# A two-layer graph attention kernel: the first layer's step with row-tiled turns and 64x64 columns

## The chip, the cores and the metric

The kernel runs on one core of a Trainium2 chip. A core has a matrix engine (TensorE, PE in the profile; its weight loads are PEld), VectorE (DVE), ScalarE (ACT), GpSimd (POOL) and SyncE (SP), which work side by side and wait for each other by semaphores. Matrix products land in PSUM, eight banks of 512 float32 columns on 128 partitions; everything else lives in SBUF or in the chip's memory, reached by DMA. The metric is the device time of one execution in microseconds.

## The reference

Eight graphs share one 2048 x 2048 adjacency matrix; every node has 64 features. Two attention layers follow one another, and a node attends only to its neighbours and itself. Then come two normalisations.

```python
def _gat_layer(h, mask, b):
    scores = jnp.einsum('...nd,...md->...nm', h, h)
    scores = jnp.where(mask, scores, NEG)
    attn = jax.nn.softmax(scores, axis=-1)
    return jnp.einsum('...nm,...md->...nd', attn, h) + b

mask = graph + jnp.eye(N) > 0
h = jnp.einsum('bnc,hdc->bhnd', x, Wh)               # 4 heads of 64
out_h = _gat_layer(h, mask, bh)                      # first layer
z = leaky_relu(concat of heads, 0.2)
h2 = jnp.einsum('bnk,dk->bnd', z, Wo)
out2 = _gat_layer(h2, mask, bo)                      # second layer
z2 = leaky_relu(out2, 0.2)
out = layernorm(z2) * gamma + beta
return layernorm(x + out)
```

The adjacency is sparse away from the first nodes: node i is linked to node j with a probability that falls with both numbers.

## The kernel before, in words

**Sets.** The first 56 nodes, the hubs, are dense and are handled against all nodes in an opening stage (0 to about 150 us). The other 1992 nodes are cut into 166 sets of 12. For each set the kernel finds at most 128 nodes that are neighbours of any of the 12 (the list of the set), and then works densely on 128 x 12 with a mask. Lists are found in three rounds of 60, 60 and 46 sets: `make_keys` turns adjacency bits into numbers, `pick` (L727) selects the 128 largest by VectorE instructions MAX8 and MATCH_REPLACE8 (`top`, L735), eight at a time, and `members` builds the masks. `pick` returns a list of jobs; `some(n)` runs the next n of them.

**The first layer's step.** 83 pairs of sets, g = 0 to 82. The loop at L1017 runs over i and each pass emits the work of several pairs at different depths of the pipeline; this order in the code is the order on each engine, since the schedule is written by hand. In pass i before the change:

- scores of pair i+1 (L814, L821): 32 products of 64x64 by 48 columns, each two passes of TensorE (a float32 product is always two, a turn one); then the mask is subtracted on VectorE (`weigh`, L826);
- the projection of pair i-1 by head (L531, 16 passes), and its bias on ScalarE (`leaky`, L518);
- ScalarE copies the turned rows of pair i+2 out of PSUM (L1030), then takes the exponential of pair i+1 (`lift`, L833);
- values of pair i (L846, 32 passes, 128 rows by 64 columns), then on VectorE the reciprocals of the sums and their product with the values (`invert`, L853 and L854);
- POOL issues two gathers (L792), one for each list, of 128 rows from a table in memory for pair i+5, and every second pass copies own features of the sets to come (`own_rows`, L800);
- the leaky part of pair i-1 on VectorE (`leak`, L523); the second layer's features of pair i-2 (`second_maps`, L880) and their copy (`keep_own`, L885); the turn of pair i-3's features into rows (`second_rows`, L890), their bias (`keep_rows`, L894) and the write to the second layer's table (L897);
- columns (L806): own features of pair i+4 multiplied by each head's Gram matrix; two products of the full 128x128 array with 192 columns, in which the Gram matrix stands twice on the diagonal; ScalarE keeps them (L812);
- the turns (L512, L863): the gathered rows of pair i+3, two times four turns of 128x128, and between the two the turn of pair i's values, four of 112x128, copied by ScalarE in two instructions (L870).

PSUM holds four tiles of two banks, one of each kind: S (scores), C (`cat`: projection, columns, second maps, second rows), O (values and their turn) and T (turned rows). A tile is taken again only when its readers have finished, and where two engines read one bank, they do so in turn.

**Selection.** Rounds two and three of `pick` run beside the first layer's step, one or two jobs a pass; a job is a MAX8 and its MATCH_REPLACE8 together. Passes below zero run none. Three more hub jobs for each of two halves (`hub_later`, L622) and the key making of round three also lie in the first passes.

**The second layer** works in 42 groups of four sets on the table that the first layer wrote: gather of 128 rows for each set (L792), the same turn (L512 from `turn2`, L1314), a copy (L1320), scores (L1133), exponential (L1136), a turn of scores (L1144), mask (L1152), values (L1165) and the normalisations on VectorE and ScalarE. The hub stage turns x with the same function (`turn_x`, L580).

## Time and profile before

| what | us |
|---|---|
| median of 14 runs | 1043.41 (1039.75 to 1050.45) |
| the profiled execution | 1040.47 |
| its span | 1038.5 |
| hub stage (to the first step's products) | 0 to about 150 |
| first layer: first scores to last scores, 83 of them | 156.4 to 612.7 |
| second layer, from the last write of rows | 629 to 1038.5 |

The busy line of the page gives each engine's busy time, its share of the span and its instructions. A line of the chain of work that ended last has the start, the length and the engine, tile and line of a piece; "issue" is time in which nothing visible was waited for, and "remote" in a timeline is a releaser that the profile couldn't name. A timeline line has start, length, engine, line, operation, output and inputs, shapes, count, and in brackets the idle time ahead of it with what ended it. PE busy counts overlapping products once.

### The profile page before, as it was taken

What the parts mean: (1) busy time and instruction counts of PE and PEld (TensorE: products, weight loads), DVE (VectorE), ACT (ScalarE), POOL (GpSimd) and SP (SyncE); (2) the same over time, 40 slices, a digit from 0 to 9 for tenths busy, and PEclk for the clock granted to TensorE, in tenths of its full rate; (3) what the DMA queues carried; (4) which work ended last, traced back from release to release, by engine and by line L of the source; (5) the groups of instructions that cost most, each with busy time, mean ns of one, the idle gap of its engine ahead of it and who ended that gap; (6) DMA issues with size and microseconds to landing.
All of it is one profiled execution on the core that took longest, in us unless ns stands there. A gap on an engine that the chain in (4) does not pass through costs nothing.

```text
span 1038.5 us, 42066 instructions
## 1 busy us (share of the span) xinstructions
PE 828.6 (80%) x18437; PEld 697.1 (67%) x18437; DVE 612.7 (59%) x1369; ACT 518.6 (50%) x961; POOL 462.9 (45%) x612
## 2 busy tenths in 40 slices
PE   3976779899999999999999983577787787777740
PEld 2654457778899888888888973366576665655540
DVE  3449735688777777555555553024454555557695
ACT  2322235555666666666666651245444544545541
POOL 6542224563444556555555515444444343545400
PEclk9999889999999999999999996799989899999985
DMA  8885513553444555555555415455555555555521
GB/s 190 230 216 153 149 26 101 151 135 95 107 115 115 144 156 150 155 144 158 149 148 153 131 33 162 141 158 151 157 158 164 150 161 151 164 159 159 164 60 32
DMA packets 81794, 145.22 MB, mean 140 GB/s; under 512 B 30146, under 2 KB 46466, under 8 KB 81602
## 3 DMA queue, kind: packets, MB, share of 16 engines
q0 software_dynamic: 26720, 88.55, 31.5%
q1 hardware_dynamic: 37842, 49.65, 16.4%
q10 hardware_dynamic: 17040, 4.25, 2.3%
q8 instruction: 147, 2.41, 1.0%
q14 instruction: 45, 0.37, 0.1%
HBM read 123.91 MB, written 18.48 MB: 137 GB/s over the span
## 4 chain that ended last, share of the span: by engine, by line
PE 65%; DVE 10%; issue 8%; ACT 7%; DMA 3%; another core or an unknown queue 3%; POOL 2%; SPq 0%; DVEq 0%; POOLq 0%; ACTq 0%
PE t L512 15%; PE s L821 10%; PE o L846 8%; PE cat L806 5%; PE s L1133 4%; PE cat L531 3%; PE o L863 3%; ACT xTg L1320 3%; PE o L1165 3%; PE cat L880 3%; PE sh L1277 2%; PE e L1144 2%; PE cat L890 2%; DMA x<-in_x_dram 1%
## 5 line engine op out<-in xcount | busy, mean ns | idle before, releaser
L792 POOL DMA_INDIRECT g<-table,index x332 | 330.1, 994 | 404.6 <-PE o L846 171.9
L512 PE MATMUL t<-ident,g 128*128 128x128 f32 x1328 | 200.6, 281 | 25.2 <-DMA gh<-table 10.8
L512 PEld LDWEIGHTS t<-ident,g 128*128 128x128 f32 x1328 | 158.8, 145 | 44.4 <-issue 36.7
L1320 ACT COPY xTg<-t 128x1024 f32<-128x1024 f32 x83 | 80.6, 1016 | 129.5 <-PE t L512 81.4
L826 DVE TENSOR_TENSOR e<-s,mask 128x768 f32<-128x768 f32 x83 | 79.4, 957 | 105.3 <-PE s L821 104.7
L821 PE MATMUL s<-y,xTg 64*64 64x48 f32 x5312 | 114.6, 222 | 4.9 <-issue 3.8
L821 PEld LDWEIGHTS s<-y,xTg 64*64 64x64 f32 x5312 | 98.6, 134 | 24.5 <-issue 16.2
L1152 DVE TENSOR_TENSOR es<-e,linked 128x384 f32<-128x384 f32 (+1 forms) x42 | 23.1, 550 | 137.3 <-PE t L512 84.8
L518 ACT ACTIVATE z<-cat,bhp 128x192 f32<-128x192 f32 x166 | 60.7, 417 | 86.0 <-PE cat L531 86.0
L846 PE MATMUL o<-g,e 128*64 128x65 f32 x2656 | 97.4, 227 | 0.0
L846 PEld LDWEIGHTS o<-g,e 128*64 128x64 f32 x2656 | 85.8, 140 | 10.0 <-issue 0.4
L1133 PE MATMUL s<-xTg,bd 128*32 128x128 f32 x1328 | 62.8, 303 | 33.0 <-issue 20.6
L1030 ACT COPY xTg<-t 128x1024 f32<-128x1024 f32 x83 | 84.0, 1012 | 1.9 <-PE t L512 1.9
L833 ACT ACTIVATE e<-e,shifts 128x768 f32<-128x768 f32 x83 | 79.2, 954 | 2.0 <-DVE e L826 2.0
L1133 PEld LDWEIGHTS s<-xTg,bd 128*32 128x32 f32 x1328 | 41.5, 120 | 49.7 <-issue 39.7
L597 ACT ACTIVATE e<-e,shifts 128x896 f32<-128x896 f32 x32 | 33.4, 1042 | 80.5 <-DVE e L594 69.2
L812 ACT COPY y<-cat 128x384 f32<-128x384 f32 (+1 forms) x80 | 40.7, 509 | 64.2 <-DVE rowt L894 42.3
L806 PE MATMUL cat<-xo,gram 128*128 128x192 f32 (+1 forms) x320 | 65.0, 326 | 0.0
L680 POOL TENSOR_SCALAR a<-raw 120x1024 bf16<-120x1024 int32 (+1 forms) x34 | 38.1, 1123 | 59.0 <-DMA raw<-in_adj_dram 31.2
L853 DVE RECIPROCAL rall<-o 64x8 f32<-64x8 f32 x166 | 34.1, 205 | 45.4 <-PE o L846 43.9
L1165 PE MATMUL o<-g,es 128*32 128x65 f32 x2656 | 54.3, 234 | 7.8 <-DVE y_s L1188 5.1
L854 DVE TENSOR_TENSOR osb<-o,rall 128x512 f32<-128x512 f32 x83 | 57.3, 691 | 2.9
(177 smaller groups left out, 1440.3 us busy)
## 6 DMA issues: line engine op xcount, KB each, us to landing
raw<-in_adj_dram SPq DMA_DIRECT2D x32, 480.0 KB
table<-xb SPq DMA_DIRECT2D x22, 256.0 KB
xr_s<-table SPq DMA_DIRECT2D x21, 256.0 KB
g<-table,index POOLq DMA_INDIRECT x332
table<-x SPq DMA_DIRECT2D x16, 260.0 KB
x<-in_x_dram ACTq DMA_DIRECT2D x32, 128.0 KB
table<-rowt SPq DMA_DIRECT2D x166, 24.4 KB
xb<-in_x_dram SPq DMA_DIRECT2D x164, 24.0 KB
```

Of the source, the lines that this page charges most:

```text
L512: nc.tensor.transpose(tp[:, q * P:(q + 1) * P], rows[:, q, 1:1 + P], ident)
L518: nc.scalar.activation(z[:, hp], cat[:, :, hp * n:(hp + 1) * n], AF.Identity, bias=bhp[:, hp:hp + 1], scale=1.0)
L792: nc.gpsimd.indirect_dma_start(out=t.rearrange("n q c -> n (q c)"), out_offset=None, in_=table, in_offset=bass.IndirectOffsetOnAxis(ap=ind ...
L806: nc.tensor.matmul(cat[:, k, 2 * GM:2 * GM + n], gram[:, g % 2 * 2 + k, :], held["x", g // 2][:, :n], start=True, stop=True)
L821: nc.tensor.matmul(sp[half(r), p, (q * 2 + j) * M:(q * 2 + j + 1) * M], xt[half(p), j, q, half(r)], y[half(p), (j * Q + q) * M:(j * Q + q ...
L826: nc.vector.tensor_tensor(e[:, :16 * M].rearrange("p (a q n) -> p a q n", a=2, q=Q), sp[:, :, :8 * M].rearrange("p a (q n) -> p a q n", q= ...
L833: nc.scalar.activation(e[:, :16 * M], e[:, :16 * M], AF.Exp, bias=shifts[:, 0:1], scale=1.0)
L846: nc.tensor.matmul(op[half(p), j, o0:o0 + K1], e[:, c0:c0 + 64], rw[j][:, q, sums(p)], start=True, stop=True)
L1030: nc.scalar.copy(t, held.pop(("tp", i + 2)))
L1133: nc.tensor.matmul(sp[q * 32:(q + 1) * 32, k, :], bd[u % 3][:, k, q, :], xt[:, s % 2, q, :], start=True, stop=True, tile_position=(0, q * 32))
L1165: nc.tensor.matmul(op[t * 32:(t + 1) * 32, f, k * W2 + p:k * W2 + p + K1], e[:, 2 * q + p, k, :], rw[:, q, sums(p)], start=(a == 0 and k = ...
L1320: nc.scalar.copy(t, tp)
```

## The change

- `turn` is row-tiled: each turn of 128 rows becomes two of 64 rows, one in each half of the array's rows, which write 64 columns each to the two banks of the tile. It is used by the first layer's step, by the hub stage and by the second layer; their readers are adapted.
- Columns are computed in 64x64 tiles without the doubled Gram matrix, 8 products of 96 columns (16 passes) instead of 2 of 192 (4 passes). They move to the O tile, just ahead of the values; `own_rows` lays own features out in two halves with partitions exchanged, by three copies instead of one.
- The turn of values moves from its own pass to the next one, to the C tile behind the projection, in 8 turns of 48 rows instead of 4 of 112; ScalarE copies it in one instruction. What follows (projection, leak, second maps, second rows) moves one pass later too, and the loop has one pass more.
- Second maps go to the S tile, behind the subtraction of the mask. The row turn becomes two turns of 64 rows.
- A selection job is split in two, MAX8 and MATCH_REPLACE8. The hub stage runs six instead of three at a time. In the step: six a pass below pass 0, three a pass up to pass 15 and two from then on, one of them between the subtraction and the leak, the others at the end of the pass behind `keep_rows`.
- Loads of own rows and their beta start at pass 10, in every third pass, instead of at pass 30 in every second.
- Order of a pass now: scores; copy of turned rows; projection; mask, exponential; columns; values; gathers; own rows; one job; second maps; leak; keep own; keep columns; invert; turn of values; second rows; keep values; keep rows; jobs; turns of gathered rows.

```diff
-    def turn(tp, rows):
+    def turn(tp, rows, j=0):
         for q in range(Q):
-            nc.tensor.transpose(tp[:, q * P:(q + 1) * P], rows[:, q, 1:1 + P], ident)
+            c0 = (j * Q + q) * 64
+            for r in range(2):
+                nc.tensor.transpose(tp[:, r, c0:c0 + 64], rows[half(r), q, 1:1 + P], ident[half(r), half(r)])
...
         def top(src, dst, last):
-            def job():
-                nc.vector.max(out=dst, in_=src)
-                if not last:
-                    nc.vector.match_replace(out=src, in_to_replace=dst, in_values=src, imm_value=-1.0)
-            return job
+            todo.append(lambda: nc.vector.max(out=dst, in_=src))
+            if not last:
+                todo.append(lambda: nc.vector.match_replace(out=src, in_to_replace=dst, in_values=src, imm_value=-1.0))
...
     def own_rows(m):
-        w = min(4, NS - 4 * m)
         t = held["x", m] = work.tile([P, 2 * GM], F32, tag="xo", name=f"xo{m}", bufs=2)
-        src = xT[:, :, HUB:].rearrange("c q (k s) -> c s q k", s=NS)[:, 4 * m:4 * m + w]
-        nc.gpsimd.tensor_copy(t[:, :w * 48].rearrange("c (s q k) -> c s q k", s=w, q=Q), src)
+        v = t.rearrange("c (b s q k) -> c b s q k", b=2, s=2, q=Q)
+        src = xT[:, :, HUB:].rearrange("c q (k s) -> c s q k", s=NS)
+        nc.gpsimd.tensor_copy(v[:, 0], src[:, 4 * m:4 * m + 2])
+        b0 = min(4 * m + 2, NS - 2)
+        for r in range(2):
+            nc.gpsimd.tensor_copy(v[half(r), 1], src[half(1 - r), b0:b0 + 2])
-    def columns(g, cat):
-        n = min(4, NS - 4 * (g // 2)) * 48
+    def columns(g, op):
+        t = held["x", g // 2]
         for k in range(2):
-            nc.tensor.matmul(cat[:, k, 2 * GM:2 * GM + n], gram[:, g % 2 * 2 + k, :], held["x", g // 2][:, :n], start=True, stop=True)
+            for r in range(2):
+                for p in range(2):
+                    nc.tensor.matmul(op[half(p), r, Q * OW + k * GM:Q * OW + (k + 1) * GM], gram[half(r), g % 2 * 2 + k, half(r)],
+                                     t[half(r), (p ^ r) * GM:((p ^ r) + 1) * GM], start=True, stop=True)
...
-    def turn_values(g, op):
-        osb = held.pop(("o", g))
+    def turn_values(g, pt):
+        osb = held.pop(("o", g)).rearrange("a j q c -> a (j q c)")
         for w in range(4):
-            nc.tensor.transpose(turned(op)[:, w, :], osb[:112, w].rearrange("a s c -> a (s c)"), ident[:112, :112])
-    def keep_values(g, op):
+            for p in range(2):
+                mine = slice(p * 64, p * 64 + M)
+                nc.tensor.transpose(pt[:, p, w * M:(w + 1) * M], osb[mine, w * P:(w + 1) * P], ident[mine, mine])
+    def keep_values(g, pt):
         ot = held["ot", g] = work.tile([P, H, GM], F32, tag="ot", name=f"otb{g}")
-        v = turned(op)
-        for p in range(2):
-            nc.scalar.copy(ot.rearrange("c h (p w n) -> c p h w n", p=2, w=4)[:, p],
-                           v[:, :, p * 64:p * 64 + M].rearrange("c w (n h) -> c h w n", h=H))
+        nc.scalar.copy(ot.rearrange("c h (p m) -> c p m h", p=2), pt.rearrange("c p (m h) -> c p m h", h=H))
...
     def second_rows(g, pr):
-        nc.tensor.transpose(pr, held.pop(("own", g)), ident)
+        t = held.pop(("own", g))
+        for r in range(2):
+            nc.tensor.transpose(pr[:, r, :], t[half(r)], ident[half(r), half(r)])
...
-    for i in range(-4, NG + 3):
+    for i in range(-4, NG + 4):
...
         cat = one(f"cat{i}", "C")
+        if 0 <= i - 2 < NG:
+            project(held.pop(("ot", i - 2)), cat, GM)
+            held["z", i - 2] = leaky(cat, GM, f"z{i - 2}")
         if 0 <= i + 1 < NG:
+            weigh(i + 1, sp)
             lift(i + 1)
+        op = one(f"o{i}", "O")
+        if 0 <= i + 4 < NG + NG % 2:
+            columns(i + 4, op)
         if 0 <= i < NG:
             values(i, op)
...
+        quota = 6 if i < 0 else 3 if i < 16 else 2
+        if not turns():
+            some(1)
+            quota -= 1
+        if 0 <= i - 3 < NG:
+            second_maps(i - 3, sp[:, 0, 384:384 + GM])
+        if 0 <= i - 2 < NG:
+            leak(held["z", i - 2])
+        if 0 <= i - 3 < NG:
+            keep_own(i - 3, sp[:, 0, 384:384 + GM])
+        if 0 <= i + 4 < NG + NG % 2:
+            keep_columns(i + 4, op)
+        if 0 <= i < NG:
+            invert(i, op)
+        if 0 <= i - 1 < NG:
+            turn_values(i - 1, cat[:, :, 2 * GM:4 * GM])
+        if 0 <= i - 4 < NG:
+            second_rows(i - 4, cat[:GM, :, 384:448])
+        if 0 <= i - 1 < NG:
+            keep_values(i - 1, cat[:, :, 2 * GM:4 * GM])
+        if 0 <= i - 4 < NG:
+            keep_rows(i - 4, cat[:GM, :, 384:448])
+        for _ in range(quota):
+            if not turns():
+                some(1)
...
+            for j in range(2):
+                turn(tp, rows[1, 2 * (i + 3) + j], j)
```

## The prediction

> **What bounds the kernel now.** I read the busy line of the page first, then busy time by stage, then the chain that ended last inside one step of the first layer, then the weight loads by shape, and last one stretch of the second layer.
>
> ```profile
> PE 828.6 (80%) x18437; PEld 697.1 (67%) x18437; DVE 612.7 (59%) x1369; ACT 518.6 (50%) x961; POOL 462.9 (45%) x612
> ...
> 262.00:600.00 338.00, 331.84 (x8581) 298.97 (x8579) 217.02 (x557) 216.24 (x437) 184.16 (x241) 1.00 0.52 141
> 629.00:1038.50 409.50, 271.37 (x5248) 220.12 (x5248) 215.91 (x393) 181.42 (x321) 163.21 (x166) 0.87 0.52 145
> ```
>
> The second and third lines are stretches of the span: PE, PEld, DVE, ACT, POOL busy, then clock, DMA share, GB/s. The 80% is a mean of two regimes. In the first layer's steps (262 to 600 us) TensorE is busy 98% at full clock; VectorE and ScalarE 64%, DMA 52%. In the second layer (from 629) TensorE is at 66%.
>
> One step of the first layer, along the chain that ended last (start, us, what):
>
> ```profile
> 310.59 1.27 PE s L821 x60
> 311.85 0.39 PE cat L531 x16
> 312.24 1.08 PE o L846 x32
> 313.32 0.33 PE cat L880 x8
> 313.65 0.24 PE cat L890
> 313.90 0.65 PE cat L806 x4
> 314.55 0.44 PE t L512 x4
> 314.99 0.39 PE o L863 x4
> 315.37 0.44 PE t L512 x4
> ```
>
> Nothing but TensorE: scores, projection, values, second maps, row turn, columns, and the turns of gathered rows around the turn of values. They add to 5.23 us, and the next scores start 5.22 us later. So here a TensorE microsecond saved is worth one, until another loop is longer.
>
> **The change, part by part.** *Price of a row-tiled turn.* A 128-column turn (L512) takes 0.44/4 = 0.109 us and one of 112 columns (L863) 0.39/4 = 0.097: 0.85 ns a moving column. A matmul is two passes: L806's 0.65/4 = 0.163 us for 192 columns is the same rate. A half turn streams 64 columns, 0.055 us, but still loads 128 stationary columns. The weight loads (min/median/max ns):
>
> ```profile
> L512 PEld LDWEIGHTS t<-ident,g x1328: 137/141/243, 152.2 to 992.3; 128*128 128x128 f32 x190
> ...
> L890 PEld LDWEIGHTS cat<-ident,own x83: 122/124/157, 185.9 to 626.7; 128*96 128x96 f32 x83
> ...
> L846 PEld LDWEIGHTS o<-g,e x2656: 132/138/231, 160.3 to 619.2; 128*64 128x64 f32 x190
> ...
> L806 PEld LDWEIGHTS cat<-xo,gram x320: 186/190/312, 161.8 to 606.8; 128*128 128x128 f32 x160
> ...
> 602.35 0.44 PE t L512 x4
> ...
> 606.73 0.42 PE cat L806 x4
> ```
>
> For turns the load grows from 122 to 137 ns between 96 and 128 columns, about 0.45 ns a column: 128 cost some 0.06 us. For matmuls it grows from 132 to 186 between 64 and 128, 0.84 ns a column; there it can bind: four passes of only 96 columns (the last line) still took 0.42 us. So a half turn costs about 0.058 us, stream and load alike. The two halves lie in different rows of the array and write different banks. That such pairs overlap is shown by the scores: 64 passes of 64x64 in 1.08 us in the step at 603.65, 0.017 each, impossible one after the other with 48 columns at 0.85 ns (0.041). No 64x128 pair is in the trace. Ends: 0.058 a pair (full overlap) and 0.116 (none). I take 0.058, the scores being the nearest row.
>
> [...]
>
> *TensorE's step anew.* Scores 1.28, projection 0.38, values 1.08 and maps 0.33 stay. Columns become 16 passes of 64x64 by 96, the form of the projection: 0.36 (was 0.65). Turn of values: 8 half turns, 4 pairs, 0.23, plus the change of array form that now falls before them (L890, one pass, took 0.24 against 0.11 streamed: 0.13): 0.36 (was 0.39). Row turn: one pair, 0.06 (was 0.24). Gathered rows: 8 pairs, 0.47 (was 0.88). Sum 4.32 us; 0.91 less.
>
> *What is late next: a loop through VectorE.* The O tile is now written by columns and values, read by ScalarE (columns kept) and then VectorE (inversion); readers of one bank go in turn, as L812 waits for L894 today. So each step has: subtraction of the mask 0.96 (L826), exponential 0.95 (L833, next in ScalarE's order), columns kept 0.51 (L812), inversion 0.42 + 0.69 (L853, L854), rows kept 0.28 (L894), the selection jobs at the step's end, and the next subtraction behind them on VectorE. With hand-overs of 0.05 (values end 313.32, L853 starts 313.37) that is 4.0 us, plus 0.49 for each trailing half job (a MAX8 and its replacement start 0.97 apart from the next pair): 4.0, 4.5 or 5.0 with none, one or two. The job between subtraction and leak is beside the exponential.
>
> Jobs: round two of the selection has 66 half jobs, round three 65. 24 go in the four steps before step 0, 48 in steps 0 to 15 (three each), the other 59 at two a step, to about step 45. So: 15 intervals at 5.0, 30 at 4.5, 37 at 4.32 (TensorE) = 370 us; 82 at 5.23 are 429. **-59 us.** What stands above 5.23 now (82 intervals between first and last scores, 156.4 to 612.7, are 456 us, 27 more: hub jobs, key making, short gaps inside the scores) I leave standing; all of it going would be -27, twice it +27.
>
> *Queues.* ScalarE: 1.01 + 0.73 + 0.95 + 0.51 + 0.51 (one copy of values' turn for two) = 3.7 us, under the step. POOL: two gathers 2.0 and their 0.3 gaps, own rows 0.28, column rows three copies every second step (0.53 becomes some 0.9), beta 1.28 in every third step instead of every second from step 10: 3.5 at most. SP issues what it did, own rows' loads 20 steps earlier. Gathers: both issued after the values, needed two steps later at the turns; 10 us of cover become 7. The two of 313.5 and 314.8 had their packets done by 318.1, 3.3 us after the second. If that cover went, each microsecond late would be a microsecond a step.
>
> *Small parts.* The turn of values moves a step later: one step more at the end, a drain of 2 to 4 us by the last intervals (4.4 to 5.0) less what overlaps: **+2.5**. Turning x in the hub stage: 16 x 0.2 off TensorE, busy 69% there: 0 to -3, **-1**. Signals from TensorE that come late (below): 0 to 0.5 us a step; I take 0.05: **+4**.
>
> *Second layer.* It uses the same turn: 83 x 0.41 = 34 us less TensorE work. Is it on the path?
>
> ```profile
> 830.18 2.47 PE L512 MATMUL t<-ident,g 128*128 128x128 f32 x16
> ...
> 832.95 0.94 POOL L792 DMA_INDIRECT g<-table,index  x1 [0.30 <-issue]
> ...
> 833.87 1.93 ACT L1320 COPY xTg<-t 128x1024 f32<-128x1024 f32 x2 [3.17 <-PE t L512]
> ...
> 837.32 2.32 PE L512 MATMUL t<-ident,g 128*128 128x128 f32 x16
> ...
> 839.62 0.94 POOL L792 DMA_INDIRECT g<-table,index  x1 [0.30 <-issue]
> ...
> 841.53 1.93 ACT L1320 COPY xTg<-t 128x1024 f32<-128x1024 f32 x2 [3.67 <-remote]
> ```
>
> The turns end at 832.65 and 839.64, yet the copy behind them starts 1.2 and 1.9 us later, each time when the fourth gather has been issued (833.89, 840.56). The gathers' series, which waits for the values, covers the turns. Ends 0 and -34; I take **-3**.
>
> **Sum.** -59 + 2.5 - 1 + 4 - 3 = -56.5. The profiled execution took 1040.47 us (span 1038.5), so 984; the median, 1043.41, stands 2.9 above it: **987 us**.
>
> **The rivals.** *Row tiles take turns.* Thirteen pairs a step at 0.116 instead of 0.058 are 1.51 us, with the 3.43 that stays or is columns and the 0.13 for the change of form 5.07: 82 x 0.16 = -13, with drain, signals and no gain elsewhere 1034 against the execution, 1037 against the median. For: no 64x128 pair in the trace. Against: the scores.
>
> *A longer loop.* If TensorE's signals come 0.5 us late at each step, subtraction and inversion shift and every interval is near 5.0: 82 x 0.23 = -19, about 1023. For: the second layer's late copies, when gathers are issued. Against: in the first layer at 313.32 the signal took 0.05.
>
> *The second layer gains too.* Were its turns on the path, -31 more: 956. For: the chain names L512 there. Against: the four lines above.
>
> *Slower.* A half turn pays a matmul's load, 0.84 ns x 128 = 0.107 us, and the halves do not overlap: 26 half turns a step are 2.78 us instead of 0.75, the step 6.34: 82 x 1.11 = +91 in the first layer, up to 83 x 0.83 = +69 in the second, so 1134 to 1203 by the median. It decides from the price where the first layer's step passes 5.2: 3.43 + 0.13 + 26 x price, so from 0.063 us for each half turn (half a pair, 0.029, is the forecast). For: L806's loads. Against: L512's.
>
> **How the numbers follow.** Forecast 0.69, its own range 965 to 1005 (the 27 us of excess by half either way, some second layer); second layer too 0.08; row tiles in turn 0.08; longer loop 0.06; slower 0.07; 0.02 is left for no change. 950 to 1030 takes in the first, second and fourth of these, some 0.8, and leaves out the slower case and the row tiles in turn. About 0.3% is what a measurement of this kernel can tell from no change. Row tiles in turn is on the edge of that bound, so a little of it counts as same. Faster 0.90, same 0.03, slower 0.07.
>
> **What would show it.** Right: first-layer scores every 4.3 to 5.0 us, shorter after step 45; eight turn passes in pairs, 16 in about 0.47; L806's successor near 0.36; VectorE as releaser of project (its cat tile) in the first 45 steps; second-layer stretch within 10 us of 409. Wrong: 16 half turns in 0.9 or more; steps above 5.0; TensorE waiting on gathers.

## The result, and the profile after

The changed kernel took 1148.99 us (median of 10 runs, 1144.59 to 1158.74), the kernel before 1043.7 (47 runs): a ratio of 1.101, 95% interval 1.098 to 1.104. It is 10% slower where 5% faster was forecast.

The first lines are the page's busy line and the first line of its chain; then the answer by stretches (span, then PE, PEld, DVE, ACT, POOL busy with instructions, clock, DMA share, GB/s), all of the changed kernel:

```profile
PE 841.4 (73%) x21252; PEld 697.4 (61%) x21252; DVE 617.3 (54%) x1369; ACT 568.6 (49%) x878; POOL 486.5 (42%) x696
...
PE 53%; issue 13%; DVE 11%; ACT 9%; another core or an unknown queue 7%; DMA 4%; POOL 1%; SPq 1%; ACTq 0%; DVEq 0%; POOLq 0%
```

```profile
262.00:600.00 338.00, 280.59 (x8513) 245.07 (x8513) 190.95 (x478) 215.62 (x315) 169.11 (x253) 0.92 0.43 118
750.80:1107.80 357.00, 265.77 (x5652) 215.27 (x5651) 179.83 (x322) 166.81 (x297) 137.98 (x142) 0.83 0.52 141
```

From 262 to 600 us TensorE was busy 331.8 us before; now it is 280.6, though only 52 steps begin in this stretch instead of 63. The step got longer, and every engine is now idle more than before. The granted clock in this stretch fell too, from 1.00 to 0.92. "issue", time in which the engine waited for nothing that the profile shows, went from 8% of the chain to 13%.

By stage (starts of the scores in the two profiled executions): the stretch from first to last scores grew from 456.3 to 531.7 us (median step 5.34 to 5.89), its start moved from 156.4 to 160.8, the passage from the last scores of the first layer to the first of the second grew from 37.4 to 58.3, the second layer's own stretch from 347.3 to 357.0, the tail from 41.1 to 43.1. That is +75, +4, +21, +10 and +2: the 112 us of the two spans.

One step in the chain that ended last (start, us, what):

```profile
405.56 0.33 PE s L888 x8
405.89 0.38 PE cat L874 x8
406.27 0.06 PE cat L900 x2
406.33 0.49 PE t L514 x16
406.82 0.61 PE s L834 x14
407.44 0.41 issue
407.85 0.35 PE s L834 x4
408.20 0.42 issue
408.62 0.88 PE s L834 x42
```

The prices are those forecast: 16 half turns 0.49 (forecast 0.47), turn of values 0.38 (0.36), row turn 0.06; the columns, 16 passes, took 0.33 a few steps later (0.36). But the scores are torn: after 14 passes TensorE stands for 0.41 us, does four passes, stands again. It waits for no semaphore there. In 262 to 600 us the records of the weight loads show 134 such gaps of over 0.15 us, 69.5 us together, 120 of them beginning within 1.3 us of the issue of a gather, moments that make up 40% of the time. Before the change there were 27, 8.1 us together, 2 of them behind a gather. The clock goes with it: it was granted at 0.50 in spells of 3.4 us or more, and the 14 steps of this stretch that such a spell touched took 8.1 us in the mean, the 38 others 5.8. Whether the clock fell because TensorE stood was not tested.

Two more lines of interest, from the page's groups and then POOL's timeline (in brackets the idle time ahead, and what ended it):

```profile
L879 ACT COPY otb<-cat 128x384 f32<-128x384 f32 x83 | 69.6, 839 | 31.3 <-PE t L514 25.2
L808 POOL COPY xo<-xT 64x96 f32<-64x96 f32 x84 | 35.9, 427 | 107.8 <-DMA g<-table,index 102.7
...
L823 ACT COPY y<-o 128x384 f32<-128x384 f32 x80 | 68.6, 857 | 19.8 <-PE o L858 18.0
```

```profile
442.30 1.15 POOL L797 DMA_INDIRECT g<-table,index  x1 [1.75 <-PE o L858]
443.76 0.95 POOL L797 DMA_INDIRECT g<-table,index  x1 [0.30 <-issue]
444.71 0.36 POOL L805 COPY xo<-xT 128x96 f32<-128x96 f32 x1
447.70 0.84 POOL L808 COPY xo<-xT 64x96 f32<-64x96 f32 x2 [2.64 <-DMA g<-table,index]
448.60 0.26 POOL L894 COPY own<-own 128x96 f32<-128x96 f32 x1
```

The exchanged copies of own rows (L808) wait until the gathers issued just ahead have landed: 2.6 us in the mean every second step, in which POOL does nothing. The straight copy L805 just ahead of them does not wait for the gathers. The two ScalarE copies take 0.86 and 0.84 us, where 0.51 was forecast for each.

At the passage to the second layer, from the timeline:

```profile
734.44 1.12 PE L514 MATMUL t<-ident,g 64*128 64x64 f32 x16 [4.17 <-issue]
...
742.96 0.94 POOL L797 DMA_INDIRECT g<-table,index  x1 [0.30 <-issue]
...
747.87 1.93 ACT L1334 COPY xTg<-t 128x1024 f32<-128x1024 f32 x2 [12.78 <-remote]
```

24 gathers follow one another there, the last issued by 743.9. TensorE's turns end at about 735.5, and the copy that needs them starts only at 747.87; ahead of these turns TensorE itself stood 4.2 us for "issue".

### The profile page after: what moved, and what is told of

The parts are those of the page before. It is cut to its first block, busy times and chain, and to the rows that moved or that the text cites. A ratio compares the mean times of both kernels' runs of the same rounds, so it can differ in the third digit from the quotient of the medians.

```text
span 1150.9 us, 47469 instructions
## 1 busy us (share of the span) xinstructions
PE 841.4 (73%) x21252; PEld 697.4 (61%) x21252; DVE 617.3 (54%) x1369; ACT 568.6 (49%) x878; POOL 486.5 (42%) x696
## 4 chain that ended last, share of the span: by engine, by line
PE 53%; issue 13%; DVE 11%; ACT 9%; another core or an unknown queue 7%; DMA 4%; POOL 1%; SPq 1%; ACTq 0%; DVEq 0%; POOLq 0%
PE s L834 11%; PE o L858 8%; PE t L514 7%; PE s L1147 4%; PE cat L537 3%; PE o L816 3%; ACT xTg L1334 3%; PE cat L874 2%; PE sh L1291 2%; DMA raw<-in_adj_dram 2%; PE o L1179 2%; PE s L888 2%; PE e L1158 2%; PE oh L615 1%
## 5 line engine op out<-in xcount | busy, mean ns | idle before, releaser
L797 POOL DMA_INDIRECT g<-table,index x332 | 322.9, 973 | 376.8 <-PE o L1179 155.4
L834 PE MATMUL s<-y,xTg 64*64 64x48 f32 x5312 | 147.2, 231 | 56.6 <-issue 55.4
L514 PE MATMUL t<-ident,g 64*128 64x64 f32 x2656 | 137.6, 239 | 59.7 <-issue 43.6
L834 PEld LDWEIGHTS s<-y,xTg 64*64 64x64 f32 x5312 | 120.5, 142 | 78.7 <-issue 71.0
L514 PEld LDWEIGHTS t<-ident,g 64*128 64x128 f32 x2656 | 111.5, 149 | 81.6 <-issue 72.5
L858 PE MATMUL o<-g,e 128*64 128x65 f32 x2656 | 113.2, 244 | 6.0 <-issue 5.9
L858 PEld LDWEIGHTS o<-g,e 128*64 128x64 f32 x2656 | 99.5, 156 | 19.3 <-issue 11.5
L879 ACT COPY otb<-cat 128x384 f32<-128x384 f32 x83 | 69.6, 839 | 31.3 <-PE t L514 25.2
L808 POOL COPY xo<-xT 64x96 f32<-64x96 f32 x84 | 35.9, 427 | 107.8 <-DMA g<-table,index 102.7
L823 ACT COPY y<-o 128x384 f32<-128x384 f32 x80 | 68.6, 857 | 19.8 <-PE o L858 18.0
L1179 PEld LDWEIGHTS o<-g,es 128*32 128x32 f32 x2656 | 61.3, 138 | 8.3 <-issue 5.5
```

The source lines that it names most:

```text
L514: nc.tensor.transpose(tp[:, r, c0:c0 + 64], rows[half(r), q, 1:1 + P], ident[half(r), half(r)])
L797: nc.gpsimd.indirect_dma_start(out=t.rearrange("n q c -> n (q c)"), out_offset=None, in_=table, in_offset=bass.IndirectOffsetOnAxis(ap=ind ...
L823: nc.scalar.copy(held["y", g // 2].rearrange("p (b n) h -> p b h n", b=2)[:, :, h0:h0 + 2, :], op[:, :, Q * OW:Q * OW + 2 * GM].rearrange( ...
L834: nc.tensor.matmul(sp[half(r), p, (q * 2 + j) * M:(q * 2 + j + 1) * M], xt[half(p), r, j, q, :], y[half(p), c0:c0 + M], start=True, stop=True)
L858: nc.tensor.matmul(op[half(p), j, o0:o0 + K1], e[:, c0:c0 + 64], rw[j][:, q, sums(p)], start=True, stop=True)
L879: nc.scalar.copy(ot.rearrange("c h (p m) -> c p m h", p=2), pt.rearrange("c p (m h) -> c p m h", h=H))
```

## The experiments

They ran on five other chips, on which the kernel before takes 878 to 880 us, not 1043. Each ratio is therefore to the kernel before on the same chip. On these chips the second layer's stretch is 215 us instead of 347, and the first layer's step of the kernel before is a flat 5.00. So they tell what the change does there; what the first result adds is taken up at the end of this section.

### First question: is it the gathers, and what of them?

Three kernels with 156 of the first layer's 166 gathers changed; all three also put a constant in place of the exponentials' argument and never set the final flag, so that only their times are to be read. In the first the gathers are left out:

```diff
+        if layer == 1 and s >= 10:
+            t = rows[layer, s] = fixed[s % 10]
+            return
```

> The changed kernel, in which the first layer gathers only its first 10 lists and reads those ten tiles again and again; the exponential there is taken of a constant so that sums stay finite, and the fallback flag is never set. Left out: 156 of 166 gathers of the first layer. Theory S (starved by gathers): TensorE's issue gaps of 0.4 us inside the scores come while a gather is generated or lands; without gathers they vanish and the step falls from 6.5 us (531.7 us from first to last scores) to 4.3 to 5.0: 360 to 410 us from first to last scores. Theory R (mean rate): TensorE gets some 50 instructions a microsecond whatever else runs (50.8 before, 50.4 after, from 262 to 600 us); then the step stays near 6.4 and the stretch near 525.

In the second SyncE moves as many bytes in a plain transfer, in the third POOL makes the same gather of 64 bytes a row:

```diff
+            nc.sync.dma_start(out=t.rearrange("n q c -> n (q c)"), in_=table[s * 11:s * 11 + P, :])
...
+            nc.gpsimd.indirect_dma_start(out=t.rearrange("n q c -> n (q c)")[:, :16], out_offset=None, in_=tiny,
+                                         in_offset=bass.IndirectOffsetOnAxis(ap=index[:, s:s + 1], axis=0))
```

> As a_gather_none, but in place of each gather left out SyncE issues one plain DMA of the same 128 rows' size (266 KB, consecutive rows of the table) into the same tile. Left out: the choice of rows. If the gather hurts TensorE by the descriptors that POOL generates, the gaps are gone as without gathers: first to last scores 360 to 410 us. If it hurts by its traffic, the gaps stay: above 470 us. Theory R: near 525.

> As a_gather_none, but each gather left out is replaced by an indirect DMA of the same 128 indices that brings 64 bytes a row in place of 2080 (from a small table written in the hub stage). [...] If POOL's descriptors starve TensorE, the stretch from first to last scores stays above 470 us; if the traffic does, it falls to 360 to 410 us. Theory R: near 525.

Measured, one execution each: 884.5, 922.3 and 882.5 us beside 880.3 for the kernel before; stretch of the scores 420, 455 and 426, so neither theory's figures came true. A plain transfer of the same bytes costs some 30 to 35 us of the stretch, and the gathers on POOL with 64 bytes a row next to nothing (6 us of the stretch, none of the time). That POOL makes descriptors, as two expectations have it, is shown by no run; the traces show its gather instruction, 0.97 us each in the changed kernel (L797). But without gathers the step is still 4.87 in the median, not 4.32. Its chain:

```profile
443.95 0.64 PE o L864 x22
444.59 0.16 PE s L894 x3
444.75 0.48 issue
445.23 0.41 PE s L894 x5
445.64 0.38 PE cat L880 x8
446.01 0.06 PE cat L906 x2
446.08 0.49 PE t L514 x16
446.57 1.08 PE s L840 x64
447.64 0.35 PE cat L537 x16
447.99 0.33 PE o L822 x16
448.32 0.20 PE o L864
448.52 0.73 issue
```

The first stop is behind the third pass of the maps, the next behind the first pass of the values, so between them lie 5 + 8 + 2 + 16 + 64 + 16 + 16 + 1 = 128 passes. A pass is two instructions, a weight load and a product (21,252 of each on the changed kernel's page). Counted over 300 to 600 us, 43 of the 44 gaps of over 0.15 us without a wait stand at the same place of a count by 256 instructions. The page's table of DMA queues (packets, MB, share) gives the other half; first the kernel before, then the changed one, both as first measured:

```profile
q8 instruction: 147, 2.41, 1.0%
```

```profile
q8 instruction: 168, 2.75, 1.0%
```

A packet has 16,384 bytes in the records. The 36,874 and 42,504 instructions of TensorE's passes, taken 256 at a time, are 144 and 166, within three of the 147 and 168 packets. From these counts and the place of the gaps I infer that TensorE's program is fetched 256 instructions at a time, a packet each, and that here it runs out. From one such packet, a fetch, to the next it takes at the least 3.2 to 3.5 us in every kernel's first layer (300 to 600 us: 3.74 in the median without gathers, 4.07 with them in the changed kernel on another chip). I call this theory F. A step of the changed kernel has 324 instructions (274 before): 324/256 x 3.74 = 4.73 us, and beside gathers 5.15.

The kernel before on these chips has no such gap at this place from 262 to 560 us; the changed one stops there at 30 of some 69 fetches, 0.17 to 1.95 us each.

### Undoing the row-tiled turns, alone and in the kernel before

All turns of rows whole again, the rest of the change kept:

```diff
-            for r in range(2):
-                nc.tensor.transpose(tp[:, r, c0:c0 + 64], rows[half(r), q, 1:1 + P], ident[half(r), half(r)])
+            nc.tensor.transpose(tp[:, j, q * P:(q + 1) * P], rows[:, q, 1:1 + P], ident)
```

> The changed kernel with the turns of 128 rows undone in all three stages (128x128 again), all else as changed. By its busy time TensorE's step is 4.32 + 0.41 = 4.73 us. Theory S: eight passes of 0.11 us each cover a gap in the supply as sixteen of 0.03 do not; the step falls from 6.5 to 5.0 to 5.6 and the second layer goes back to within 10 us of before: 1010 to 1070 us in all. Theory R: 308 instructions a step instead of 324 at 50 a microsecond, 6.1 us: the first layer gives back 25 us and the second 30: 1090 to 1100.

924.9 us, ratio 1.048 (1.044 to 1.052), the second layer 217.7. Both theories had been given in times of the first result, so the total decides between neither. The median step of 5.25 is no better than the 5.28 of the changed kernel below, though a step has 16 instructions fewer: the turns stream longer again (1.02 us a step where they took 0.49), and TensorE also waits for POOL's exchanged copies of own rows (13.5 us from 262 to 560). On another chip the changed kernel itself, the kernel before, and the kernel before with only the row-tiled turn:

> The changed kernel itself, on the chip of this call, where the kernel before took 880 us in the call before this one instead of 1043. If TensorE's supply is what slows the change (theory S), a chip on which the second layer's steps are faster with the same code should show fewer issue gaps and a ratio nearer to 1: 0.95 to 1.06. If the change is slower for a reason inside the step that has nothing to do with the chip's state (a longer loop through ScalarE and VectorE), the ratio stays at 1.10.

> The kernel before itself, for its profile on the same chip as the others of this call. Both theories: first-layer steps of 5.2 us where TensorE binds.

> The kernel before with one part of the change: row-tiled turns of 128 rows in all three stages, all else as before. TensorE's step is 0.41 us shorter by busy time. Theory S: the queue's stock of long passes shrinks from 12 turns of 0.11 us to 16 half turns of 0.03, so issue gaps show in the scores and the step gets no shorter than 5.2 or longer; without supply trouble on this chip it is 4.9 and the first layer gains up to 30 us. A loop elsewhere: no gain and no gaps.

The changed kernel took 930.3, ratio 1.056 (1.049 to 1.064), with irregular steps (median 5.28, mean 5.73) and the second layer at 225.0 against 215.4. The kernel before repeated itself: 880.1, steps of 5.00. With the row-tiled turn alone it took 896.9, ratio 1.017 (1.009 to 1.024): the step became 5.05. Eight half turns took 0.39 us where four whole ones took 0.44, twice a step, but the turn of values between them, its own form unchanged, went from 0.39 to 0.53; I put that down to the other form of the turns around it, which was not tested by itself. The second layer lost 10 us. The change, then, is slower by 5 to 6% there too, and row-tiled turns are a loss to the second layer.

Where TensorE stands in the changed kernel on this chip can be read from its weight loads. From 262 to 560 us there are 30 stops without a wait at one place of the 256 instructions, 19.5 us, and waits for the exchanged copies of own rows, from the answer on waits (sum, times, longest in us):

```profile
PEld o L816 <- POOL xo L808: 17.8, 26, 2.8
```

The kernel before has neither. That is 0.36 and 0.33 us a step, in steps whose mean grew from 5.05 to 5.46: the shorter streaming makes up for a part only. In the second layer there are 13 stops at that place, 11.2 us, and with the row-tiled turn alone 15, 14.6 us, where the kernel before has one of 0.7: of the size of the 10 us lost.

### Supply measured by itself

Two series of 1536 products of 64x64 by 8 columns behind all work of the kernel before:

```diff
+        for k in range(n):
+            r, p = k % 2, k // 2 % 2
+            nc.tensor.matmul(ps[half(p), r, 0:8], ident[half(r), half(p)], ident[half(r), 0:8], start=True, stop=True)
```

> The kernel before, with two series of 1536 matmuls of 64x64 by 8 columns behind all its work, which change nothing of the output; 24 gathers of 128 rows are issued beside the second series. 3072 instructions a series are 12 fetches of 16 KB in the records of the instruction queue. Theory F (TensorE's instructions come 256 at a time, one fetch after the other, and the shortest distance seen between two fetches is 3.3 us): the first series takes 12 x 3.4 to 3.8 = 41 to 46 us, the second 12 x 4.0 to 4.4 = 48 to 53 us or more. Without such a limit: at most 1536 x 0.017 (the scores' pass, which has more columns) = 26 us, both series alike. Theory S (TensorE starves while gathers land): first series 26 us, second 50 or more.

The expectation had forgotten that each of these products is two passes (768 products were 1,534 in the records of the second kernel's first series, below): each series is 24 fetches, not 12. In the records of weight loads TensorE stood at a multiple of 128 passes again and again, 0.24 to 0.52 us each time before the gathers and up to 1.06 beside them; 20 lots of 256 instructions took 74.9 us, 3.75 each, before the gathers, and 8 lots took 32.7, 4.09 each, beside them. A second kernel measured four series, small products alone and beside 24 gathers, then 400 whole turns alone and beside 24 gathers.

> The kernel before with four series behind all its work, which change nothing of the output: 768 matmuls of 64x64 by 8 columns (1536 passes, 3072 instructions, 12 fetches) alone, the same beside 24 gathers, 400 whole turns of 128x128 alone, the same beside 24 gathers. By the supply measured before: small alone 12 x 3.75 = 45 us, beside gathers 47 to 49. Whole turns at 0.109 us: 44 us, alone and beside gathers, since 800 instructions in 44 us are far under the supply. If gathers also stop TensorE's instructions for some 0.55 us or more each, as the records of the changed kernel suggest where the kernel before takes 1040 us: small beside gathers 60 us or more, whole turns beside gathers less than 10 us longer; where the kernel before takes 880 no such stop.

Answer by stretches, one line for each series:

```profile
854.50:897.10 42.60, 41.61 (x1534) 41.33 (x1532) 12.34 (x20) 3.29 (x9) 0.00 (x0) 0.50 0.11 22
897.20:944.50 47.30, 42.68 (x1543) 41.84 (x1540) 0.26 (x2) 0.00 (x0) 22.70 (x24) 0.50 0.49 139
944.80:990.30 45.50, 45.50 (x402) 45.50 (x399) 0.00 (x0) 0.00 (x0) 0.00 (x0) 0.95 0.01 1
990.40:1034.00 43.60, 43.60 (x402) 43.60 (x401) 0.26 (x2) 0.00 (x0) 22.67 (x24) 1.00 0.52 148
```

Gathers lengthen the small passes by 4.7 us (11%) and the whole turns not at all; within the second series a lot takes up to 4.57 us, within the first 3.41 to 4.02. One thing limits these lines as a measure of supply: the granted clock was 0.50 in both series of small products, and a pass then takes 0.027 us, so that 256 instructions need 3.4 us already for that.

### POOL's wait, and the forms, one by one

Theory W: POOL's wait for the gathers just issued makes the next gathers late. First, own rows ahead of the step's gathers:

```diff
+        if i + 6 < NG and i % 2 == 0 and i >= -2:
+            own_rows((i + 6) // 2)
         if 0 <= i + LOOK < NG and i > -3:
             for j in range(2):
                 gather(table1, 2 * (i + LOOK) + j, 1, rows_tile)
-        if i + 6 < NG and i % 2 == 0 and i >= -2:
-            own_rows((i + 6) // 2)
```

> The changed kernel, with the copies of own rows ahead of the step's two gathers on POOL instead of behind them, nothing else. Theory W (POOL's exchanged copies wait for the gathers just issued, some 2.4 to 3.5 us every second step, and POOL's loop of 5.3 us a step is the bound): first-layer step from a median of 5.28 to some 4.8, stretch between first and last scores from 470 to 420 to 435, ratio to before from 1.056 to 1.00 to 1.02. Theory F alone (instruction fetches slowed by the gathers' traffic): stretch 460 to 470, ratio 1.045 to 1.056. Theory A (the loop through VectorE and ScalarE with its longer copies): step 5.0 and above, ratio 1.03 to 1.05.

921.4, ratio 1.046 (1.041 to 1.051), median step 5.24: near nothing of what W promised. On POOL the edit did not do what it was for, since POOL runs so late that the last gathers were issued just ahead all the same:

```profile
439.15 0.95 POOL L797 DMA_INDIRECT g<-table,index  x1 [0.30 <-PE t L514]
440.12 1.28 POOL L938 TENSOR_TENSOR xb<-xb,bet 128x512 f32<-128x512 f32 x1
441.35 0.26 POOL L894 COPY own<-own 128x96 f32<-128x96 f32 x1
441.56 0.34 POOL L805 COPY xo<-xT 128x96 f32<-128x96 f32 x1
444.35 0.76 POOL L808 COPY xo<-xT 64x96 f32<-64x96 f32 x2 [2.45 <-DMA g<-table,index]
```

POOL's wait fell only from 131 to 101 us in sum. But TensorE's wait for these copies (17.8 us) is gone from the answer on waits, and the stops at the one place of the 256 instructions went from 30, 19.5 us, to 56, 38.4 us. So one limit stood behind the other: what TensorE no longer waits for POOL, it now mostly waits for its instructions. On the same chip, the same with whole turns in the second layer only, and with whole turns in both layers (edits as above):

> As the one with own rows first, and the second layer turns its rows whole (128x128) as before the change. Row-tiled turns cost the second layer some 8 to 10 us by an earlier run on the kernel before. Expected: first layer as with own rows first, second layer 215 to 218 instead of 225, ratio 0.01 below it: 0.99 to 1.01 by theory W, 1.035 to 1.045 by the others. If row-tiled turns are free in the second layer: no difference.

> As the one with own rows first, but all turns of rows whole, in both layers: 16 instructions fewer in a first-layer step (some 308 instead of 324) and 0.41 us more of streaming. Theory F (a step of 324 instructions is 1.27 fetches at 3.74, 4.7 us; with 308 1.20, 4.5): the same time as with turn2 alone, within 6 us, first-layer step 4.7 to 4.9. If TensorE's streaming sets the step: 82 x 0.41 = 34 us more than with turn2 alone.

913.8, ratio 1.036 (1.029 to 1.043), second layer 215.4; and 897.5, ratio 1.019 (1.014 to 1.024). The second one gives TensorE half a microsecond more of turns in each step (1.02 us where 0.49 was), and the median step falls from 5.33 to 5.01, the stretch by 16 us. More streaming does not explain that, 16 instructions fewer by theory F do: the stops at that place go from 51, 43.7 us, to 21, 10.9 us.

The opposite test, a dose of useless passes ahead of the scores of the kernel with own rows first and whole turns, and of the kernel before (n = 4 or 12 products, two passes each):

```diff
+        for k in range(n):
+            r, p = k % 2, k // 2 % 2
+            nc.tensor.matmul(sp[half(p), r, 480:488], ident[half(r), half(p)], ident[half(r), 0:8], start=True, stop=True)
```

> The kernel with own rows first and all turns whole (ratio 1.019 to before, first-layer step 5.01 in the median, 308 TensorE instructions), and in each first-layer step 4 more matmuls of 64x64 by 8 columns ahead of the scores into columns that nobody reads: 8 passes, 16 instructions, some 8 x 0.017 = 0.14 us of streaming at most. Theory F (256 instructions take 4.09 us while gathers run, from the second series measured): 324 instructions are 5.18 us a step, +0.26: 83 x 0.26 = +21 us, ratio 1.04. If TensorE's streaming sets the step: +11 us, ratio 1.03. If neither (waits for gathers, copies of ScalarE): no change.

> The same with 12 matmuls, 24 passes, 48 instructions, at most 0.41 us of streaming. Theory F: 356 instructions are 5.69 us a step: +0.77 to the one without them, +64 us, ratio 1.09. Streaming: +34 us, ratio 1.06. Neither: no change.

> The kernel before with the same 4 matmuls a first-layer step as the first of these runs: 294 instructions instead of 278, by theory F 4.70 us of supply under a step of 5.0, so only streaming counts: +0 to +11 us, ratio 1.00 to 1.013, and half or less of what the same 16 instructions cost in the changed kernel. If small instructions cost the same everywhere: +21, ratio 1.024.

The median step of the changed kernel went from 5.01 (measured on another chip) to 5.24 and 5.69 (F: 5.18 and 5.69), that of the kernel before from 5.00 to 5.11. In time the small dose does not tell them apart: ratio 1.036 (1.030 to 1.043), which is +0.017 for the changed kernel, and 1.017 (1.012 to 1.023) for the kernel before, where up to 1.013 was expected. The large dose costs +0.059 (1.078, 1.072 to 1.084), 52 us, between streaming (34) and F (64), nearer F.

Then the columns undone alone, in the O tile ahead of the values, with the straight copy of own rows (no wait on gathers), and whole turns in the second layer:

```diff
+        nc.gpsimd.tensor_copy(t[:, :w * 48].rearrange("c (s q k) -> c s q k", s=w, q=Q), src)
...
+            nc.tensor.matmul(op[:, k, Q * OW:Q * OW + n], gram[:, g % 2 * 2 + k, :], held["x", g // 2][:, :n], start=True, stop=True)
```

> The changed kernel with the columns undone alone (4 passes of 128x128 by 192 beside the values instead of 16 of 64x64 by 96, one copy of own rows on POOL without exchange, ScalarE's copy of the columns as before), and whole turns in the second layer. 300 instructions a step: theory F 4.80 us; streaming 4.32 + 0.29 and two more changes of array form, 4.6 to 4.9; POOL's loop without the wait for gathers. Expected by F and W together: first-layer step 4.8 to 4.95 in the median, second layer 215, ratio 0.99 to 1.01. By F without W, or if the wait is not what costs: as with own rows first, 1.02 to 1.036.

893.2, ratio 1.013 (1.008 to 1.019), median step 4.81, many of 4.62 to 4.65. That is 300 instructions; F gives 4.8. The ratio is not what was expected: it lies between the two ranges given. With whole turns in the first layer too, 284 instructions:

> The changed kernel with the columns undone and all turns of rows whole in both layers: 284 instructions a first-layer step, 4.54 us of supply beside gathers, under a streaming sum of 4.32 + 0.29 + 0.41 = 5.02 and changes of array form. Theory F: steps near 5.05, steadier than with 300 instructions; what is left above the kernel before is not supply (later turn of values with one step more, order of the queues): ratio 1.005 to 1.02. If waits on gathers or on VectorE were the limit in the kernels with fewer fetches too: irregular steps as before, ratio as with the columns undone alone, 1.013, or above 1.02.

899.7, ratio 1.024 (1.020 to 1.029). From the 18th interval between scores on, all are 5.15 us but one (6.76) and the last three, and this piece of the chain has no "issue":

```profile
441.95 1.02 PE t L512 x8
442.98 1.08 PE s L825 x64
444.05 0.35 PE cat L535 x16
444.40 0.85 PE o L809 x4
445.25 1.08 PE o L849 x32
446.33 0.33 PE s L879 x8
446.66 0.38 PE cat L865 x8
447.04 0.06 PE cat L891 x2
```

1.02 + 1.08 + 0.35 + 0.85 + 1.08 + 0.33 + 0.38 + 0.06 = 5.15. Here supply would take 4.54 and streaming takes 5.15, so streaming rules, and the step is as steady as before the change. Put beside each other, for steps that start between 262 and 560 us (instructions counted from the weight loads, two for each; a stop is a gap of over 0.15 us between weight loads, without a wait, at the one place of the 256):

| kernel | instructions a step | median step | us for 256 | stops, us in them |
|---|---|---|---|---|
| no gathers | 324 | 4.84 | 3.82 | 42, 20.5 |
| gathers of 64 bytes a row | 324 | 4.77 | 3.77 | 36, 15.3 |
| plain transfers for gathers | 324 | 5.27 | 4.16 | 49, 42.8 |
| changed kernel, on these chips | 324 | 5.27 | 4.16 | 30, 19.5 |
| own rows first | 324 | 5.19 | 4.10 | 56, 38.4 |
| own rows first, second layer whole | 324 | 5.29 | 4.18 | 51, 43.7 |
| own rows first, all turns whole | 308 | 4.96 | 4.12 | 21, 10.9 |
| the same, 8 passes added | 324 | 5.23 | 4.13 | 29, 15.8 |
| the same, 24 passes added | 356 | 5.67 | 4.08 | 30, 24.8 |
| changed kernel, all turns whole | 308 | 5.17 | 4.30 | 9, 3.6 |
| columns undone | 300 | 4.75 | 4.05 | 18, 9.0 |
| columns undone, selection jobs whole (below) | 300 | 4.79 | 4.09 | 16, 8.2 |
| columns undone, all turns whole | 284 | 5.15 | 4.64 | 1, 0.2 |
| kernel before | 274 | 5.00 | 4.67 | 0, 0.0 |
| kernel before, 8 passes added | 290 | 5.11 | 4.51 | 4, 2.2 |
| kernel before, row-tiled turns | 290 | 5.05 | 4.46 | 4, 2.3 |

Eight kernels with gathers, 300 to 356 instructions a step, lie at 4.05 to 4.18 us for 256, as does the one with plain transfers; the two without that traffic at 3.77 to 3.82. One is off this line: the changed kernel with all turns whole, at 4.30, where TensorE waits for POOL as said above. Those whose streaming takes longer than the supply have next to no such stops. The third figure only divides the second by the first; the stops are the direct sign.

Last, the selection jobs whole again, in the kernel with the columns undone:

```diff
-            todo.append(lambda: nc.vector.max(out=dst, in_=src))
-            if not last:
-                todo.append(lambda: nc.vector.match_replace(out=src, in_to_replace=dst, in_values=src, imm_value=-1.0))
+            todo.append(job)
...
-        quota = 6 if i < 0 else 3 if i < 16 else 2
+        quota = 3 if i < 0 else 2 if i < 16 and i % 2 == 0 else 1
```

> The changed kernel with the columns undone, whole turns in the second layer, and the selection jobs whole again (half as many each step). If the loop through VectorE (subtraction, exponential, inversion, trailing jobs) sets early steps: up to 15 x 0.49 = +7 us to the same kernel with halved jobs, ratio 1.02. If not (as its early steps of 4.62 with three halves a step suggest): the same within 5 us, ratio 1.013.

877.9, ratio 0.9997 (0.997 to 1.003): 1.3% better than with halved jobs (on another chip), against both expectations. In the profiled executions the first scores come at 152.6 instead of 161.8, and the third to fifth interval take 6.33, 6.24 and 6.47 instead of 8.31, 7.75 and 7.10. The earlier start can't be put down to the jobs: the other kernels with halved jobs have their first scores anywhere from 149.0 to 161.8 us. Why halves are dearer in the early steps was not tried. This is the best version found: equal to the kernel before, better than the changed one, and not a gain.

### What stays open

The first result. The record does not name its chip; from the times I take it for another one than the five. There TensorE stands for 0.4 to 0.6 us, mostly twice, behind each pair of gathers, at any place in the 256 instructions, and in 262 to 600 us the median distance of fetches is 4.90 us, so the fetch is not what runs out. On the other chips such stops are few: 19 within 1.3 us of a gather in the changed kernel, 10.2 us, of which 9, 7.3 us, at the fetch's place. The kernel before has them in its second layer: 120 stops without a wait, 54.1 us, 108 of them within 1.3 us of a gather, on the first result's chip, against a single one on another. Two lines show these stretches; the first is the first result's chip, the second one of the others:

```profile
650.10:997.40 347.30, 257.48 (x5017) 208.53 (x5016) 179.24 (x322) 170.38 (x298) 149.40 (x153) 0.92 0.56 154
```

```profile
620.00:835.00 215.00, 201.33 (x5026) 185.03 (x5025) 177.60 (x323) 170.04 (x296) 156.54 (x155) 1.00 0.83 251
```

The same 5,020 passes and the same work of VectorE and ScalarE, in 347 and in 215 us. No run of mine landed on a chip like the first. So that the gathers cause these stops is read from when they begin, and was not tested. Why one chip has them and five have not is unknown, and so is why the kernel before has next to none in its first layer on the same chip, with as many gathers. Nor is it separated how much the lower clock (0.92 against 0.97 on another chip, 262 to 600 us) adds to the first result by itself.

## Why the prediction was wrong, point by point

- **Price of a row-tiled turn**: right. 16 half turns in 0.49 us, 0.061 a pair (forecast 0.058). The halves overlap: each took 0.031 us, where 64 columns at the turns' 0.85 ns would stream in 0.055. The rival that they take turns (0.116 a pair) falls, and so does the slower rival, by whose load of 0.107 us for each half 16 of them would take 1.7 us one after the other. The change came out slower all the same, by another way; that the slower rival's range of 1134 to 1203 holds the measured time is luck.
- **TensorE's step anew, "Sum 4.32 us; 0.91 less"**: the sum is right: six steps of the changed kernel on another chip, between 270 and 590 us, take 4.31 to 4.33. That it is right to the hundredth is luck, since the starts of the parts in such a step give 1.16 for scores (forecast 1.28), 0.44 for columns (0.36) and 0.59 for the turns of gathered rows (0.47). That it becomes the step is wrong, and this is the step of the prediction that failed. It counted passes by their streaming and never by their number. The change takes 0.9 us of streaming out of the step and puts 50 instructions in (274 to 324). On the chips of the experiments the median step is then 5.28: the supply of instructions gives 5.15 by theory F, and with POOL's copies put ahead, so that TensorE does not wait for them, it is still 5.24. Instead of -59, the stretch of the scores grew by 37 there (433.2 to 470.1), and by 75 in the first result.
- **"Signals from TensorE that come late: 0 to 0.5 us a step; I take 0.05: +4"**: this is the term that was mis-sized in the first result. The trace of before showed the late signals in the second layer, and the prediction priced them as late signals only. They go with stops of TensorE itself: 69.5 us of 338, 1.3 us a step at a mean step of 6.45. What causes these stops stays open. The prediction also left the clock at full, as it was before; it was granted at 0.92.
- **Loop through VectorE, 4.0, 4.5 or 5.0**: not seen as a limit. With three half jobs a step, where 5.0 was forecast, the kernel with the columns undone has five steps of 4.62 to 4.67 among its first 15, about what TensorE's streaming gives there (4.32 + 0.29). That the readers of one tile go in turn shows in the trace of after: VectorE's reciprocals (L865) sat idle 23.4 us, 55 times, until ScalarE's copy of the columns (L823) was done. Two of the loop's terms were wrong: ScalarE's copy of the columns takes 0.86 and that of the values' turn 0.84, not 0.51. The row used (L812, 0.513) had the same size but another pattern of access.
- **Queues, "POOL: column rows three copies ... 3.5 at most"**: the copies' time was right, their wait was missed. The prediction named no wait for them; they wait for the gathers just issued, 2.6 us in the mean every second step in the first result and 3.1 on another chip, and hold back own's copy, the next gathers and, there, TensorE's columns (17.8 us from 262 to 560). What this costs by itself is not separated: with the copies ahead TensorE no longer waits for them but stops more for its instructions, and undoing the columns removed the wait together with 24 instructions.
- **Selection jobs**: halving them was costed at nothing beyond the loop. Undoing it gave 1.3%, on another chip than the run it is compared with.
- **Second layer, "Ends 0 and -34; I take -3"**: wrong sign, and the end above nothing was left out with no reason. Measured +10 in the first result, +10 to +15 on the other chips (225.0 and 230.3 against 215.4 with whole turns), and +21 more in the passage to it on the first chip. That shorter turns gain nothing there was right; that they would then cost nothing was not: on the other chips TensorE stops for its instructions there (11.2 us in the changed kernel, 0.7 before). The late copies that were read as cover by the gathers belong to the first result: the idle time ahead of them is 129.5 us there (L1320, kernel before) and 17.7 on another chip.
- **Drain +2.5, hub stage -1**: the tail is 2 us longer; the first scores came 4 us later instead of 1 us earlier.

## What to carry to other kernels

Count instructions as well as streaming. Before cutting passes into halves, divide TensorE's instructions in a step by the step, and compare with what the same kernel reaches at best: here 256 instructions took 3.75 us without gathers' traffic and 4.1 with it, so that a step of 324 comes to about 5.2 at this rate, where its streaming sums to 4.32; one of 274 comes to 4.4, under its streaming of 5.0. "issue" pieces inside a run of small passes, at equal distances of passes (128 here), were the sign. And when a copy is split, ask anew what each part waits for (here 2.6 us for the gathers, every second step); a wait that is taken away can uncover the next limit, as when 17.8 us of waits for POOL went and the stops at the fetch's place rose from 19.5 to 38.4 us.

## What was unexpected in the hardware

- TensorE's instructions, counted 256 at a time, are 144 and 166 in the two kernels, beside 147 and 168 packets of the instruction queue; two fetches in a first layer were never closer than 3.2 us, and without gathers 43 of 44 gaps without a wait stood at the same place in the 256.
- The same kernel took 1043 us in the first result and 878 to 880 on five other chips.
- The granted clock was 0.50 in the series of 64x64 by 8 columns, and 0.95 to 1.00 in the series of whole turns right behind it.
- Four turns of 112x112, unchanged themselves, took 0.53 us between row-tiled turns and 0.39 between whole ones.
